# A two-layer graph network: GpSimd's tile operations moved to VectorE, target scores spread through DRAM, and half of each graph layer moved into the turn before

## Chip, cores, metric

One Trainium2 chip, one core, all data in float32. The metric is the device time of one execution in microseconds (us).

## The reference

128 graphs of 128 nodes with 256 features. Layer 0 is attention with relation-dependent values (8 heads) and a feed-forward; layer 1 is two graph-attention steps and a feed-forward. Four layer norms in all. What matters here of layer 1:

```python
Wh  = h @ W
e   = leaky_relu(Wh @ a[:F] + swapaxes(Wh @ a[F:], 1, 2), 0.2)   # target score + source score
att = softmax(where(adj > 0, e, NEG), axis=1)
h   = att @ Wh                                                    # done twice, then residual and norm
```

The edge tile has one graph's source nodes on the 128 partitions. A source score is then one number per partition, which an activation takes as its bias. A target score must be laid along the free axis and be the same on every partition: it has to be *spread*. How that is done is one part of the change.

## The kernel before

Four graphs make a group of 512 tokens; the 32 groups run as *turns* in a software pipeline. While one group is in the second feed-forward, the next but one is in projections and attention, and so on. Functions are generators, and an explicit order says after how many feed-forward steps the next piece of another group is issued. TensorE and ScalarE follow that order; VectorE and the rest are placed by the framework's own scheduling.

```python
def normed(t, n, mv=None):                      # statistics on VectorE
    ...
    nc.gpsimd.tensor_tensor(rs, rs, k.mhalf, op=ALU.pow)
    ...
def scaled(y, gr, br, n, o=None):               # 128x1024 each, on GpSimd
    nc.gpsimd.tensor_mul(o, y, over(gr))
    nc.gpsimd.tensor_add(o, o, over(br))
...
# scores(S, p): four times per half of a group
nc.scalar.activation(e[:, s], pss[s], AF.Exp, scale=SCALE)
nc.vector.tensor_mul(pm[:, s], e[:, s], ad[...])             # pm
# attended(S, p): sums over e and pm
nc.tensor.matmul(pav[...], v[:, d0 : d0 + DH], m[:, s, u, c, :], ...)   # m is e, then pm
...
# layer1(S): spread of target scores by matmul
nc.tensor.matmul(pb, wb[:, c, :], yT[:, c, :], ...)           # first graph step, two of these
nc.tensor.matmul(pb[:, b * P : (b + 1) * P], wh[:, b, D + 1 : D + 2].to_broadcast([P, P]),
                 att[:, b, :], start=True, stop=True)         # second graph step, four of these
# edges(): ends with
nc.gpsimd.tensor_mul(s, s, rd[:, :, None].to_broadcast([P, G, P]))
```

Of the kernel before, what the change touches and what calls it, by code (L numbers as in the profile page):

```python
# [9 lines left out]
F32 = mybir.dt.float32  # L10
I32 = mybir.dt.int32
AF = mybir.ActivationFunctionType
ALU = mybir.AluOpType
# [10 lines left out]
P = 128  # L24
# [79 lines left out]
def fast_pass(ctx, tc, a, out):  # L104
# [21 lines left out]
    small = ctx.enter_context(tc.tile_pool(name="small", bufs=4))  # L126
    ps_s = ctx.enter_context(tc.tile_pool(name="ps_s", bufs=4, space=PSUM))
# [74 lines left out]
    NU = D + 3  # L202
    wu = k.tile([P, NCH, NU], "wu")
    wb = k.tile([P, NCH, P], "wb")

    def graph_weights():
# [8 lines left out]
        gw1T = cut(NCH, D)  # L215
        for m in range(NCH):
            pt = mm_tile(f"pgt_{m}")
            for c in range(NCH):
                nc.tensor.transpose(
                    pt[:, c * P : (c + 1) * P], gw1[:, c, m * P : (m + 1) * P], k.ident  # L220
                )
            nc.scalar.copy(gw1T[:, m, :], pt[:, :D])
        yield
        for m in range(NCH):
            pu = mm_tile(f"pgw_{m}")
            for c in range(NCH):
                nc.tensor.matmul(
                    pu[:, : D + 2], gw1T[:, c, m * P : (m + 1) * P], rhs[:, c, :],
                    start=(c == 0), stop=(c == NCH - 1),
                )  # L230
            nc.scalar.copy(wu[:, m, : D + 2], pu[:, : D + 2])
            nc.vector.tensor_copy(wu[:, m, D + 2 :], wa1[:, m, 1:2])
            nc.vector.tensor_copy(wb[:, m, :], wa1[:, m, 0:1].to_broadcast([P, P]))
# [10 lines left out]

    def normed(t, n, mv=None):

        st = small.tile([P, G, 6], F32, tag="st", name="st_" + n)
        if mv is None:
            mv = small.tile([P, G, 2], F32, tag="mv", name="mv_" + n)
        for b in range(G):  # L250
            nc.vector.bn_stats(st[:, b, :], t[:, b, :])  # L251
            nc.vector.bn_aggr(mv[:, b, :], st[:, b, :])
        rs = small.tile([P, G], F32, tag="rs", name="rs_" + n)
        nc.vector.tensor_scalar(rs, mv[:, :, 1], EPS, None, op0=ALU.add)  # L254
        nc.gpsimd.tensor_tensor(rs, rs, k.mhalf, op=ALU.pow)  # L255
        for b in range(G):
            nc.vector.tensor_scalar(  # L257
                t[:, b, :], t[:, b, :], mv[:, b, 0:1], rs[:, b : b + 1],
                op0=ALU.subtract, op1=ALU.mult,
            )  # L260

    def scaled(y, gr, br, n, o=None):
        if o is None:
            o = w3p.tile([P, G, D], F32, tag="res", name="res_" + n)
        nc.gpsimd.tensor_mul(o, y, over(gr))
        nc.gpsimd.tensor_add(o, o, over(br))
        return o
# [15 lines left out]
    def added(t, p, po, res):  # L283

        nc.vector.tensor_add(  # L285
            flat(t[:, 2 * p : 2 * p + 2, :]), po, flat(res[:, 2 * p : 2 * p + 2, :])
        )

    def ffn(S, layer, inT, wa, ba, func, wb_, res):

        n = f"{layer}_{S['g']}"
# [10 lines left out]
        S[f"t{layer}"] = t = w3p.tile([P, G, D], F32, tag="t", name="t_" + n)  # L302
        for p in range(G // 2):
# [10 lines left out]
            added(t, p, po, res)  # L314
            yield

    def in_order(ffn_, *steps):


        for s in steps:  # L320
            if isinstance(s, int):
                for _ in range(s):
                    next(ffn_, None)
            elif callable(s):
                s()
            else:
                next(s, None)
        for _ in ffn_:
            pass

    def scores(S, p):

        qT, kT, ad = S["qT"], S["kT"], S["ad"]
        n = f"{S['g']}_{p}"

        pss = [ps_s.tile([P, 2, NCH, P], F32, tag="s", name=f"ps_{n}_{s}") for s in range(HC)]
        for u in range(2):
            bs = slice((2 * p + u) * P, (2 * p + u + 1) * P)
            for c in range(NCH):
                for s in range(HC):  # L340
                    rows = slice(s * DH, (s + 1) * DH)
                    nc.tensor.matmul(  # L342
                        pss[s][:, u, c, :], kT[rows, c, bs], qT[rows, c, bs],
                        start=True, stop=True,
                    )
        e = w2p.tile([P, HC, 2, NCH, P], F32, tag="e", name="e_" + n)
        pm = w2p.tile([P, HC, 2, NCH, P], F32, tag="pm", name="pm_" + n)
        for s in range(HC):
            nc.scalar.activation(e[:, s], pss[s], AF.Exp, scale=SCALE)  # L349
            nc.vector.tensor_mul(  # L350
                pm[:, s], e[:, s],
                ad[:, 2 * p : 2 * p + 2, None, :].to_broadcast([P, 2, NCH, P]),
            )
        S["e", p], S["pm", p] = e, pm

    def attended(S, p):

        e, pm, oT, g = S["e", p], S["pm", p], S["oT"], S["g"]
        n = f"{g}_{p}"
        pav = ps_av.tile([P, 2, NCH, P], F32, tag="av", name="pav_" + n)  # L360
        pden = ps_av.tile([P, 2, NCH, P], F32, tag="den", name="pden_" + n)
        for s in range(HC):
            nc.tensor.matmul(  # L363
                pden[s * DH : (s + 1) * DH], k.ones, e[:, s], start=True, stop=True
            )
        for u in range(2):
            v = S["v", 2 * p + u]
            for c in range(NCH):
                for r, m in enumerate((e, pm)):
                    for s in range(HC):  # L370
                        d0 = r * D + c * P + s * DH
                        nc.tensor.matmul(  # L372
                            pav[s * DH : (s + 1) * DH, u, c, :],
                            v[:, d0 : d0 + DH], m[:, s, u, c, :],
                            start=(r == 0), stop=(r == 1),
                        )
        den = pden.rearrange("p u c i -> p (u c i)")
        rd = w1p.tile([P, 2, NCH, P], F32, tag="rd", name="rd_" + n)
        nc.vector.reciprocal(rd, pden)  # L379
        for u in range(2):  # L380
            bs = slice((2 * p + u) * P, (2 * p + u + 1) * P)
            nc.vector.tensor_mul(oT[:, :, bs], pav[:, u], rd[:, u])
        nc.vector.tensor_reduce(c_att[:, 0, g, p : p + 1], den, AX.X, ALU.min)
        nc.vector.tensor_reduce(c_att[:, 1, g, p : p + 1], den, AX.X, ALU.max)

    def projections(S):

        g, xt, ad, xr = S["g"], S["xt"], S["ad"], S["xr"]
        n = str(g)
        nc.gpsimd.tensor_add(xr, xr, over(bo))  # L390

        scr = w2p.tile([P, G, P], F32, tag="gs", name="scr_" + n)
# [3 lines left out]
        )  # L396
        for o, w, bias in (("qT", wq, bq), ("kT", wk, bk)):
# [20 lines left out]

    def attention(S):
# [3 lines left out]
        scores(S, 0)  # L423
        yield
        attended(S, 0)
        scores(S, 1)
        yield
        attended(S, 1)
        yield
        S["t0"] = t = w3p.tile([P, G, D], F32, tag="t", name="t_0_" + n)  # L430
        for p in range(G // 2):
# [8 lines left out]
            added(t, p, po, S["xr"])  # L440
            yield

    def edges(pb, bias, S, l):

        n = f"{S['g']}_{l}"
        s = w2p.tile([P, G, P], F32, tag="gs", name="gs_" + n)
        for b in range(G):
            nc.scalar.activation(  # L448
                s[:, b, :], pb[:, b * P : (b + 1) * P], AF.Identity, bias=bias(b)
            )  # L450
        nc.vector.scalar_tensor_tensor(s, s, ALPHA, s, op0=ALU.mult, op1=ALU.max)  # L451
        nc.scalar.activation(s, s, AF.Exp)
# [9 lines left out]
        nc.gpsimd.tensor_mul(s, s, rd[:, :, None].to_broadcast([P, G, P]))  # L462
        return s

    def layer1(S):



        n, yT = str(S["g"]), S["x2T"]
# [9 lines left out]
        pb = ps_av.tile([P, T], F32, tag="den", name="pb_" + n)  # L479
        for c in range(NCH):  # L480
            nc.tensor.matmul(pb, wb[:, c, :], yT[:, c, :], start=(c == 0), stop=(c == NCH - 1))  # L481
        yield
        att = edges(pb, lambda b: wh[:, b, D + 2 : D + 3], S, 0)
        yield
        yh = w1p.tile([P, G, D + 1], F32, tag="yh", name="yh_" + n)
        pb = ps_av.tile([P, T], F32, tag="av", name="pb2_" + n)
        for b in range(G):
            py = ps_s.tile([P, T], F32, tag="s", name=f"py_{n}_{b}")
            nc.tensor.matmul(  # L489
                py[:, : D + 1], att[:, b, :], wh[:, b, : D + 1], start=True, stop=True  # L490
            )
            nc.scalar.copy(yh[:, b, :], py[:, : D + 1])
            nc.tensor.matmul(  # L493
                pb[:, b * P : (b + 1) * P], wh[:, b, D + 1 : D + 2].to_broadcast([P, P]),
                att[:, b, :], start=True, stop=True,
            )
        att = edges(pb, lambda b: yh[:, b, D : D + 1], S, 1)
        yield
        S["t2"] = t = w3p.tile([P, G, D], F32, tag="t", name="t_2_" + n)
# [473 lines left out]
```

## Time and profile before

| | before |
|---|---|
| median time | 3084.3 us (3 runs, 3083.71 to 3085.99) |
| span of the profiled run | 3083.0 us |
| TensorE, VectorE, GpSimd busy | 3007.7, 1478.7, 895.5 us |
| one turn (start of `pb` to the next) | 94.87 us |

The engine lines, the chain of waits, TensorE's waits and two timelines are shown in the prediction below.

### The profile page before, as it was taken

How to read it: one execution, taken by the hardware profiler on the slowest of the kernel's cores; microseconds unless marked ns; L12 is line 12 of the kernel's file. 1: busy time of each engine (PE TensorE's matmuls, PEld its weight loads, DVE VectorE, ACT ScalarE, POOL GpSimd, SP SyncE). 2: the span in 40 equal slices, each digit the busy share in tenths (PEclk: the TensorE clock that was granted, in tenths of full speed). 3: DMA queues.
4: the chain of work that ended last, by engine and by line, in shares of the span. 5: the costliest groups of instructions: out<-in, count | busy, mean ns of one | idle time of the engine just before them, and what ended most of it. 6: DMA issues, size and time to landing. Idle time of an engine off the chain costs nothing.

```text
span 3083.0 us, 39531 instructions
## 1 busy us (share of the span) xinstructions
PE 3007.7 (98%) x16526; PEld 1981.4 (64%) x16526; DVE 1478.7 (48%) x3445; ACT 998.4 (32%) x1735; POOL 895.5 (29%) x489
## 2 busy tenths in 40 slices
PE   8999999999999999999999999999999999999998
PEld 4666666666666666666666666666666666666665
DVE  4445543455544455444554345553445544455433
ACT  2333333333333333333333333233333333333332
POOL 1233232232232322323323223223232232332332
PEclk9999999999999999999999999999999999999999
DMA  5000000000000000000000000000000000000000
GB/s 159 18 21 18 25 18 18 21 25 18 18 23 19 21 18 18 25 18 21 18 25 18 18 21 25 18 18 23 20 21 18 18 25 18 21 18 11 8 8 15
DMA packets 58136, 69.59 MB, mean 23 GB/s; under 512 B 6752, under 2 KB 44768, under 8 KB 57952
## 3 DMA queue, kind: packets, MB, share of 16 engines
q1 hardware_dynamic: 57120, 66.61, 7.1%
q8 instruction: 131, 2.15, 0.3%
q10 hardware_dynamic: 832, 0.40, 0.0%
q14 instruction: 53, 0.43, 0.0%
HBM read 50.22 MB, written 16.78 MB: 22 GB/s over the span
## 4 chain that ended last, share of the span: by engine, by line
PE 90%; DVE 7%; DMA 1%; ACT 1%; POOL 0%; issue 0%; SPq 0%; ACTq 0%; DVEq 0%; POOLq 0%
PE po L308 29%; PE ph L296 28%; PE pq L402 7%; DVE pm L350 7%; PE pw L474 4%; PE pv L412 4%; PE pav L372 3%; PE pwo L436 3%; PE ps L342 2%; PE pt L275 2%; PE py L489 2%; PE pb L481 2%; PE pg L504 2%; PE pden L363 1%; PE pb L493 1%; ACT e L349 1%
## 5 line engine op out<-in xcount | busy, mean ns | idle before, releaser
L255 POOL TENSOR_TENSOR rs<-rs,mhalf 128x4 f32<-128x4 f32 x127 | 129.1, 1016 | 1274.7 <-DVE rs L254 1274.7
L296 PE MATMUL ph<-yT,w_L_gnn_w_ff 128*128 128x512 f32 x1024 | 462.5, 600 | 0.4 <-ACT hT L300 0.4
L296 PE MATMUL ph<-yT,w_L_gnn_W 128*128 128x512 f32 x1024 | 451.7, 592 | 3.8 <-ACT hT L300 3.4
L308 PE MATMUL po<-w_L_gnn_W,hT 128*128 128x256 f32 x2048 | 453.5, 379 | 0.0
L308 PE MATMUL po<-w_L_gnn_w_ff,hT 128*128 128x256 f32 x2048 | 452.5, 379 | 0.0
L308 PEld LDWEIGHTS po<-w_L_gnn_W,hT 128*128 128x128 f32 x2048 | 386.5, 190 | 64.8 <-issue 15.0
L308 PEld LDWEIGHTS po<-w_L_gnn_w_ff,hT 128*128 128x128 f32 x2048 | 386.7, 190 | 52.2 <-issue 1.0
L296 PEld LDWEIGHTS ph<-yT,w_L_gnn_W 128*128 128x128 f32 x1024 | 194.2, 190 | 235.8 <-issue 227.0
L296 PEld LDWEIGHTS ph<-yT,w_L_gnn_w_ff 128*128 128x128 f32 x1024 | 189.9, 190 | 213.4 <-issue 205.8
L350 DVE TENSOR_TENSOR pm<-e,adj 128x512 f32<-128x512 f32 x256 | 293.2, 1203 | 35.3 <-ACT e L349 35.3
L451 DVE SCALAR_TENSOR_TENSOR gs<-gs 128x512 f32<-128x512 f32 x64 | 44.6, 697 | 533.1 <-ACT gs L448 533.0
L300 ACT ACTIVATE hT<-ph,c_L_gnn_b 128x512 f32<-128x512 f32 x256 | 175.7, 687 | 379.0 <-PE ph L296 378.9
L300 ACT ACTIVATE hT<-ph,c_L_gnn_b_ff 128x512 f32<-128x512 f32 x256 | 176.4, 690 | 372.7 <-PE ph L296 372.7
L285 DVE TENSOR_TENSOR t<-po,res 128x512 f32<-128x512 f32 x128 | 88.5, 691 | 422.6 <-PE po L308 422.6
L462 POOL TENSOR_TENSOR gs<-gs,gr 128x512 f32<-128x512 f32 x64 | 66.7, 1042 | 699.0 <-DVE gr L461 699.0
L379 DVE RECIPROCAL rd<-pden 128x512 f32<-128x512 f32 x64 | 214.4, 3350 | 70.8 <-PE pden L363 70.8
L412 PE MATMUL pv<-wv,xT 128*128 128x512 f32 x512 | 238.7, 599 | 0.8 <-DVE v L416 0.8
L278 ACT ACTIVATE yT<-pt,c_L_gnn_beta,c_L_gnn_g 128x512 f32<-128x512 f32 x128 | 92.7, 774 | 434.6 <-PE pt L275 434.5
L349 ACT ACTIVATE e<-ps 128x512 f32<-128x512 f32 x256 | 132.2, 602 | 217.8 <-PE ps L342 217.8
L251 DVE BATCH_NORM_STATS2 st<-t 128x6 f32<-128x256 f32 x508 | 192.4, 415 | 7.4
L257 DVE TENSOR_SCALAR t<-t,mv,rs 128x256 f32<-128x256 f32 x384 | 132.7, 409 | 112.1 <-POOL rs L255 112.1
L372 PE MATMUL pav<-pm,v 128*32 128x128 f32 x2048 | 132.1, 273 | 40.4 <-DVE pm L350 40.4
(110 smaller groups left out, 3697.8 us busy)
## 6 DMA issues: line engine op xcount, KB each, us to landing
xT<-in_xT_dram SPq DMA_DIRECT2D x32, 512.0 KB, 3.7
x<-in_x_dram SPq DMA_DIRECT2D x32, 512.0 KB, 3.8
out_dram<-t SPq DMA_DIRECT2D x31, 512.0 KB, 2.9
adj<-in_adjT_dram SPq DMA_DIRECT2D x32, 256.0 KB, 2.7
w_L_gnn_W<-in_L_gnn_W_dram SPq DMA_DIRECT2D x2, 1024.0 KB, 7.6
w_L_gnn_w_ff<-in_L_gnn_w_ff_dram SPq DMA_DIRECT2D x2, 1024.0 KB, 8.7
wv<-in_L_gnn_Wv_dram SPq DMA_DIRECT2D x2, 256.0 KB, 5.2
temp<-in_L_gnn_W_dram SPq DMA_DIRECT2D x2, 256.0 KB, 5.8
```

The lines of the kernel that those rows point to most:

```text
L251: nc.vector.bn_stats(st[:, b, :], t[:, b, :])
L255: nc.gpsimd.tensor_tensor(rs, rs, k.mhalf, op=ALU.pow)
L257: nc.vector.tensor_scalar(t[:, b, :], t[:, b, :], mv[:, b, 0:1], rs[:, b : b + 1], op0=ALU.subtract, op1=ALU.mult,)
L296: nc.tensor.matmul(ph, wa[:, c, f * P : (f + 1) * P], inT[:, c, :], start=(c == 0), stop=(c == NCH - 1),)
L300: nc.scalar.activation(hT[:, f, :], ph, func, bias=ba[:, f : f + 1])
L308: nc.tensor.matmul(po[:, s * D : (s + 1) * D], hT[:, f, b * P : (b + 1) * P], wb_[:, f, :], start=(f == 0), stop=(f == NF - 1),)
L349: nc.scalar.activation(e[:, s], pss[s], AF.Exp, scale=SCALE)
L350: nc.vector.tensor_mul(pm[:, s], e[:, s], ad[:, 2 * p : 2 * p + 2, None, :].to_broadcast([P, 2, NCH, P]),)
L372: nc.tensor.matmul(pav[s * DH : (s + 1) * DH, u, c, :], v[:, d0 : d0 + DH], m[:, s, u, c, :], start=(r == 0), stop=(r == 1),)
L379: nc.vector.reciprocal(rd, pden)
L402: nc.tensor.matmul(pq, w[:, c, m * P : (m + 1) * P], xt[:, c, :], start=(c == 0), stop=(c == NCH - 1),)
L412: nc.tensor.matmul(pv, xt[:, c, b * P : (b + 1) * P], wv[:, c].rearrange("p r d -> p (r d)"), start=(c == 0), stop=(c == NCH - 1),)
```

## The change

The intent: take the broadcast products off TensorE; take all tile work off GpSimd, beside which VectorE's `pm` is slow (the prediction shows it), and give it to VectorE; and arrange VectorE by hand so that it copes. The core of the diff:

```diff
+    dram = ctx.enter_context(tc.tile_pool(name="dram", bufs=2, space=bass.MemoryType.DRAM))
-    NU = D + 3
+    NU = D + 4                                  # the target score as one more column of the product
-    wb = k.tile([P, NCH, P], "wb")
...
+    def scaled(S, i, p):                        # on VectorE, half a group at a time
+        nc.vector.tensor_mul(o[:, pair(p)], t[:, pair(p)], over(rows[i][0], 2))
+        nc.vector.tensor_add(o[:, pair(p)], o[:, pair(p)], over(rows[i][1], 2))
...
+    def spread(columns, n):
+        pr = ps_av.tile([P, P], F32, tag="den", name="pr_" + n)
+        nc.tensor.transpose(pr[:G, :], columns, k.ident)
+        nc.vector.tensor_copy(line, pr[:G, :])
+        nc.sync.dma_start(hbm, line)                      # 2 KB out
+        nc.sync.dma_start(t, hbm.partition_broadcast(P))  # 256 KB back, same on all partitions
...
-        nc.gpsimd.tensor_mul(s, s, rd[:, :, None].to_broadcast([P, G, P]))
+        nc.vector.tensor_mul(s, s, rd[:, :, None].to_broadcast([P, G, P]))
...
-    with tc.manual_schedule(engines={mybir.EngineType.PE, mybir.EngineType.Activation}):
+    with tc.manual_schedule(engines={ET.PE, ET.Activation, ET.DVE, ET.SP}):
...                                              # steady turn, f1/f2 first/second feed-forward of two groups,
                                                 # l1 graph layer, at attention, pr projections, n0..n3 norms
+    n3, f1, l1, f1, n3, l1, f1, (n3, 2), store, (f1, 2), prepared,
+    (f1, 3), (l1, 2), (f1, 5), l1, n2, (f1, 2), n2, f1, n1,
+    (pr, 2), n1, turned, pr, (n2, 2), pr, turned,
+    l1 = layer1(S1);  pr, l1, n1, pr, n1, l1, (pr, 2)     # the NEXT group's graph layer begins here
+    (f2, 2), l1, f2, l1, f2, at, (f2, 2), at, (f2, 3), at, (f2, 2), at, f2, at, n0, f2, ...
```

GpSimd keeps the power of the norm (128x4).

## The prediction

> **What bounds the kernel now.** I read the page first: its engine shares, its chain of work that ended last. Then the waits of TensorE alone, then the instruction groups by form, then timelines of one turn in mid-run. (A turn is one group of four graphs; there are 32.)
>
> ```profile
> PE 3007.7 (98%) x16526; PEld 1981.4 (64%) x16526; DVE 1478.7 (48%) x3445; ACT 998.4 (32%) x1735; POOL 895.5 (29%) x489
> PE 90%; DVE 7%; DMA 1%; ACT 1%; POOL 0%; issue 0%; SPq 0%; ACTq 0%; DVEq 0%; POOLq 0%
> ```
>
> TensorE is busy 98% of the span, and the chain is TensorE with a small share of VectorE. So only two things can shorten this kernel: matmul time taken away, or the 75 us in which TensorE stands still (3083.0 - 3007.7). The waits of TensorE say where those lie:
>
> ```profile
> PE pav L372 <- DVE pm L350: 40.4, 62, 1.1
> PE pt L275 <- DVE t L257: 11.1, 3, 6.1
> PE pq L402 <- DMA w_L_gnn_Wq<-in_L_gnn_Wq_dram: 5.9, 1, 5.9
> PE pflag L639 <- DVE good L637: 5.6, 1, 5.6
> ```
>
> The first comes back in nearly every turn (62 of 64 attention halves); the rest are the start, the end and three places without neighbouring work. Why does `pm` come late? It is the product of exponentials and adjacency, 128x512, four in a row per half. Its shortest is 674 ns, its median 680, its longest 2862, its mean 1203. The timelines of VectorE and GpSimd at one such place:
>
> ```profile
> 1501.41 2.48 DVE L350 TENSOR_TENSOR pm<-e,adj 128x512 f32<-128x512 f32 x4
> ...
> 1583.16 6.95 DVE L350 TENSOR_TENSOR pm<-e,adj 128x512 f32<-128x512 f32 x4 [1.02 <-ACT e L349]
> ...
> 1583.38 2.79 POOL L266 TENSOR_TENSOR res<-res,r_L_gnn_b_ln 128x1024 f32<-128x1024 f32 x1
> 1586.13 2.83 POOL L266 TENSOR_TENSOR res<-res,r_L_gnn_beta 128x1024 f32<-128x1024 f32 x1
> ```
>
> With GpSimd idle, four take 2.48 us; with two GpSimd additions on the same stretch they take 6.95 us, and the additions themselves stretch from 2.36 us to 2.8. TensorE pays there 1.12 + 0.19 us. A second look, for the matmuls that the change removes, on TensorE's timeline of the same turn:
>
> ```profile
> 1543.25 3.66 PE L474 MATMUL pw<-wu,yT 128*128 128x259 f32 x16
> 1546.75 1.88 PE L481 MATMUL pb<-yT,wb 128*128 128x512 f32 x4
> 1548.47 3.60 PE L296 MATMUL ph<-yT,w_L_gnn_W 128*128 128x512 f32 x8
> ...
> 1558.81 0.60 PE L489 MATMUL py<-wh,gs 128*128 128x257 f32 x2
> 1559.24 0.38 PE L493 MATMUL pb<-gs,wh 128*128 128x128 f32 x2
> 1559.46 0.60 PE L489 MATMUL py<-wh,gs 128*128 128x257 f32 x2
> ...
> 1571.78 1.89 PE L504 MATMUL pg<-yh,gs 128*128 128x256 f32 x8
> 1573.51 3.60 PE L402 MATMUL pq<-xT,w_L_gnn_Wk 128*128 128x512 f32 x8
> ```
>
> Take starts, not durations, since neighbours overlap. Each logical f32 matmul is two records.
>
> **What the Trainium skill says.** "SBUF — State Buffer", section "Who interferes with whom": a VectorE instruction with two SBUF inputs contends with a GpSimd instruction that reads SBUF; whoever starts first holds the pair for the whole instruction. `pm` and the GpSimd additions are such instructions, and 2.48 against 6.95 us agrees in direction; the GpSimd side was stretched only from 2.36 to 2.8. "GPSIMD Engine Reference", section "4.1 Engine selection": elementwise work on a tile belongs on VectorE, GpSimd being about 2 times slower with two inputs. The trace has 2.35 us for 128x1024 on GpSimd against two 128x512 of 0.62 to 0.68 us on VectorE: 1.7 to 1.9 times. "DMA: Bandwidth & Descriptors", section "Anatomy of one DMA — SWDGE (gpsimd) path": a transfer has a fixed cost of about 2.0 us, most of it the receipt of the write. Here the queue is SyncE's, but the trace is near: 1.8 us from issue to landing for the 128 KB output pieces, 2.7 us for 256 KB of adjacency.
>
> **The change, part by part.**
>
> *Removed: broadcast of target scores.* The product with a spread column `wb` (four records) goes from 1546.75 to 1548.47: 1.72 us per turn, 55.0 us in 32 turns. The second, in layer two, sits between the `py`: the four pairs take 1558.81 to 1561.43 = 2.62 us, while the like-shaped `pg` alone takes 1571.78 to 1573.51 = 1.73 us; so 0.89 us per turn, 28.5 us. The group sums of the page (60.1 and 49.2 us) are larger because they count overlaps; I do not use them. Sum: **-83.5 us**.
>
> *Added on TensorE.* Two transposes per turn of a 128x4 column block. The eight `pt` transposes in the same trace take 1528.62 to 1529.50, 0.11 us each; so 64 x 0.11 = 7 us, and I allow 2 us for the lone small weight load. One more column in `pw` and `py`: 768 records x about 0.85 ns (0.437 us per 512 columns) = 0.7 us. Sum: **+10 us**.
>
> *GpSimd tile operations to VectorE.* GpSimd keeps only the tiny power (128x4). Then nothing holds `pm` back: I expect four in 2.5 us everywhere, and the 40.4 us of waiting go: **-40.4 us**, if the order leaves no other wait there. VectorE's load: 2 (bias) + 16 (four norms, two halves, multiply and add) + 2 (edge normalisation) = 20 instructions of 128x512 per turn, 640 in all, x 0.62 to 0.68 us = about 410 us, plus 64 small copies of about 0.2 us = 13 us; saved in `pm`: 293.2 - 64 x 2.48 = 134 us. New sum 1478.7 + 423 - 134 = about 1768 us, 59% of the span. On average far from binding; it costs nothing unless a burst makes TensorE wait.
>
> *Target scores through DRAM.* Per layer: transpose 0.11, copy 0.2, two transfers one behind the other with issue (0.4 each): 1.8 + 2.7 + 0.8, about 5.6 us altogether. Cover on TensorE in the new order: layer one has two projection steps and two feed-forward steps before the edges, 4 x 1.72 = 6.9 us; layer two has six feed-forward steps, 10.3 us. Hidden, but layer one with only 1.3 us to spare, and VectorE must have copied promptly: its queue then holds a scaling and a `v` addition.
>
> *Order fixed on VectorE and SyncE; first graph layer a turn earlier.* No work is added. The edge chains (score, exponential, mask, normalise) get their feed-forward neighbours; normalised tiles are prepared a few steps before the transposes. Tightest is attention: from scores to the transposes of its norm I count some 24 us of VectorE work (pm 2 x 2.5, reciprocal 2 x 3.35, products and reductions 2 x 2.0, three additions with statistics 3 x 1.75, norm with power 2.9) inside about 30 us of matmuls. I allow 0.2 us of new wait per turn: **+6 us**. The end: in the last turn the second edge chain and its norm stand with less beside them (spread 5.6 plus chain about 6 against three steps 5.2; then a norm); I allow **+5 us**. The start has one gain (one adjacency check no longer stands inside the first norm) and one risk (graph weights in fixed order ahead of the first `v`): 0.
>
> Sum: 3084.3 - 83.5 + 10 - 40.4 + 6 + 5 = **2981 us**; per steady turn, 94.87 us (between two `pb` starts, 313.37 and 408.24) become about 91.4.
>
> **The rivals.**
> (a) *VectorE's fixed order turns into new waits.* In the kernel before, VectorE was free to be arranged otherwise and still served TensorE everywhere but in one place. With 20 more instructions per turn and an 80% full attention stretch (24 of 30 us), a late `pm`, or sum buffers freed late by the reductions (there is one of each), could cost 0.7 us per turn: 2981 + 16 = about 2997; with 1.5 us, about 3022. For: the estimate of the stretch. Against: `pm` is ahead of reciprocals in the new order.
> (b) *The DRAM route is exposed.* If the two transfers take 8 us rather than 5.3, ScalarE, which works in order, stands at the edges and its outputs free the two feed-forward accumulators late. About 1.5 us per turn after its slack is eaten: again about 3020.
> (c) *The matmuls removed were cheaper than they look, or the wait merely moves to other late `pm`.* If the 40.4 us stay, as ScalarE's exponentials or the chain in front take the blame: about 3020. Against: the longer pm coincide with GpSimd instructions.
> (d) *All is covered*, no new wait and a quiet end: about 2966.
>
> **Range and chances.** The removal of 73 us net of matmul time is arithmetic on a saturated engine, and alone gives 3011, 2.4% faster. To stay within 2% (above 3022.6), the waits would have to be 42 us longer than my sum has them: rivals (b) or (c) in full, or two together. I keep most weight between (d) and the mild (a): predicted 2981 us, range 2961 to 3008; faster by over 2%: 0.91, within 2%: 0.08, slower: 0.01.
>
> **What would show each step.** In the changed profile: TensorE's busy sum near 2935 us with share 98 to 99%; no group for `pb`, and 64 transposes into `pr` of about 0.1 us spacing; `pm` mean near 680 ns with longest below 1 us; wait of `pav` for `pm` below 10 us; GpSimd below 150 us busy, nearly all power; VectorE 1.7 to 1.8 ms; SyncE's two transfers for each spread landing in 2 and 3 us; ScalarE not waiting for a transfer at the edges. The prediction is wrong if `pm` stays above 1 us without GpSimd work beside it, if TensorE's waits name VectorE for over 40 us in sum, or if ScalarE's wait for the spread tile shows up each turn.

## More of the kernel before

One more view belongs here: busy time in a stretch in mid-run. The columns are length, then busy us (and instructions) of PE, PEld, DVE, ACT and POOL, then granted clock, DMA share and GB/s. TensorE stands still for 3.93 us in 300 us (300.00 - 296.07), by the records.

```profile
900.00:1200.00 300.00, 296.07 (x1605) 195.12 (x1604) 147.48 (x354) 96.27 (x168) 87.97 (x49) 1.00 0.07 20
```

## The result

The median fell from 3085.1 us (the 3 runs above and a fourth, 3083.71 to 3085.99) to 2958.99 us (4 runs, 2958.13 to 2959.66). The ratio is 0.9591, 95% interval 0.9575 to 0.9608. Ratios here are the mean time of one kernel's fast runs over that of the other's of the same rounds, so not quite the ratio of the medians. The gain is 126 us. I had forecast 103 (2981 us, range 2961 to 3008): right direction, but 2 us below my range.

The page of the changed kernel, engine lines and chain:

```profile
PE 2913.6 (99%) x16206; PEld 1921.8 (65%) x16206; DVE 1804.7 (61%) x4139; ACT 984.1 (33%) x1733; POOL 132.2 (4%) x137
PE 97%; DVE 2%; DMA 0%; issue 0%; ACT 0%; POOL 0%; ACTq 0%; DVEq 0%; POOLq 0%
```

The waits of TensorE in the changed kernel (for whom: us in total, times, longest):

```profile
PE pt L253 <- DVE t L291: 10.7, 4, 4.3
PE pq L393 <- DMA w_L_gnn_Wq<-in_L_gnn_Wq_dram: 6.0, 1, 6.0
PE pg L568 <- DVE gs L533: 5.3, 1, 5.3
PE pflag L682 <- DVE good L680: 4.9, 1, 4.9
PE pden L447 <- DVE c_att L472: 4.7, 2, 3.2
```

`pav` waiting for `pm` is gone; what is left lies at the start and the end: between 170 and 2864 us no wait of TensorE is listed. In a stretch of 300 us in mid-run it has no recorded gap at all, although VectorE does 43 us more in it than in the stretch of 300 us shown for the kernel before:

```profile
1000.00:1300.00 300.00, 300.00 (x1702) 201.39 (x1701) 190.18 (x432) 98.97 (x175) 14.11 (x14) 1.00 0.08 25
```

The shape of `pm` (VectorE, tile view: shortest, median and longest of 256), before and then after:

```profile
L350 DVE TENSOR_TENSOR pm<-e,adj x256: 674/680/2862, 24.8 to 2926.5; 128x512 f32<-128x512 f32 x128
```

```profile
L435 DVE TENSOR_TENSOR pm<-e,adj x256: 679/684/693, 26.3 to 2809.6; 128x512 f32<-128x512 f32 x128
```

A turn now takes 90.38 us (start of `pr` for `wh` at 256.51 and at 346.89) against 94.87. I had said 91.4. So the missing microsecond is inside each turn. The timelines of TensorE at the attention sums of one late half before show where. The columns are start, length, line, operation, tiles, and in brackets the recorded wait:

```profile
1587.83 0.40 PE L372 MATMUL pav<-e,v 128*32 128x128 f32 x8
1588.05 0.39 PE L372 MATMUL pav<-pm,v 128*32 128x128 f32 x4
1589.56 0.41 PE L372 MATMUL pav<-pm,v 128*32 128x128 f32 x2 [1.12 <-DVE pm L350]
1590.16 0.30 PE L372 MATMUL pav<-pm,v 128*32 128x128 f32 x1 [0.19 <-DVE pm L350]
...
1591.81 1.17 PE L342 MATMUL ps<-qT,kT 32*128 32x128 f32 x32
```

and at a like half after, where nothing waits:

```profile
1547.70 0.40 PE L456 MATMUL pav<-e,v 128*32 128x128 f32 x8
1547.92 0.40 PE L456 MATMUL pav<-pm,v 128*32 128x128 f32 x8
...
1549.56 3.72 PE L342 MATMUL po<-w_L_gnn_w_ff,hT 128*128 128x256 f32 x16
```

From the first `pav` to the next other work it is 1591.81 - 1587.83 = 3.98 us before and 1549.56 - 1547.70 = 1.86 us after: 2.12 us lost per late half. The brackets hold only 1.12 + 0.19 = 1.31 us. The rest is hidden: a `pav` matmul is drawn 273 ns long, while in a free run eight of them start within 0.22 us, so each wait is recorded only from the drawn end of the matmul in front of it. (The 62 waits of the list are two in each of 31 late halves; the other half of each turn takes 1.86 us in both kernels.) I added these start-to-start times over all attention halves: 185.3 us before, 121.9 us after. **The late `pm` cost 63.4 us, not the 40.4 us that the list of waits shows.**

The Trainium skill has this, and I had not looked there: "Perfetto Trace Analysis", section "Tensor Engine Instruction (MATMUL, LD_WEIGHTS)", says that the end of a TensorE instruction is estimated from its size and not observed, so its time is a model. The traces here agree, and 23 us hung on it.

### The profile page after: what moved, and what is told of

It reads as the page before. It is cut to its first block, busy times and chain, and to the rows that moved or that the text cites. A ratio compares the mean times of both kernels' runs of the same rounds, so it can differ in the third digit from the quotient of the medians.

```text
span 2957.8 us, 39390 instructions
## 1 busy us (share of the span) xinstructions
PE 2913.6 (99%) x16206; PEld 1921.8 (65%) x16206; DVE 1804.7 (61%) x4139; ACT 984.1 (33%) x1733; POOL 132.2 (4%) x137
## 4 chain that ended last, share of the span: by engine, by line
PE 97%; DVE 2%; DMA 0%; issue 0%; ACT 0%; POOL 0%; ACTq 0%; DVEq 0%; POOLq 0%
PE ph L331 30%; PE po L342 30%; PE pv L403 7%; PE pq L393 7%; PE pw L544 4%; PE pav L456 4%; PE pwo L494 4%; PE pt L253 3%; PE ps L421 2%; PE pden L447 2%; PE py L556 2%; PE pg L568 2%; DMA temp<-in_L_gnn_a_dram 0%; PE pr L504 0%; DVE rd L462 0%; DMA r_L_gnn_bo<-in_L_gnn_bo_dram 0%
## 5 line engine op out<-in xcount | busy, mean ns | idle before, releaser
L342 PE MATMUL po<-w_L_gnn_w_ff,hT 128*128 128x256 f32 x2048 | 470.3, 381 | 0.0
L407 DVE TENSOR_TENSOR v<-pv,r_L_gnn_bv 128x512 f32<-128x512 f32 x128 | 87.7, 686 | 219.9 <-PE pv L403 219.9
L277 DVE BATCH_NORM_STATS2 st<-t 128x6 f32<-128x256 f32 x512 | 210.2, 410 | 8.8
L397 ACT ACTIVATE qT<-pq,c_L_gnn_bq 128x512 f32<-128x512 f32 x64 | 44.0, 688 | 436.4 <-PE pq L393 436.4
L435 DVE TENSOR_TENSOR pm<-e,adj 128x512 f32<-128x512 f32 x256 | 159.6, 685 | 5.2 <-ACT e L427 5.1
L403 PEld LDWEIGHTS pv<-wv,xT 128*128 128x128 f32 x512 | 92.5, 190 | 93.6 <-issue 88.4
```

The lines of the kernel that those rows point to most:

```text
L277: nc.vector.bn_stats(st[:, s, :], t[:, 2 * p + s, :])
L342: nc.tensor.matmul(po[:, s * D : (s + 1) * D], hT[:, f, b * P : (b + 1) * P], wb_[:, f, :], start=(f == 0), stop=(f == NF - 1),)
L403: nc.tensor.matmul(pv, xt[:, c, b * P : (b + 1) * P], wv[:, c].rearrange("p r d -> p (r d)"), start=(c == 0), stop=(c == NCH - 1),)
L435: nc.vector.tensor_mul(pm[:, s], S["e", p][:, s], S["ad"][:, pair(p), None, :].to_broadcast([P, 2, NCH, P]),)
```

## The experiments

The theory: the gain is matmul time removed (about 73 us) plus the full delay of `pm` (63 us), less some microseconds at the ends; the other parts of the change gain nothing by themselves but keep the two from being eaten by new waits. The rivals: the recorded waits are all there was and another part gave the rest; or the order, not GpSimd's absence, cured `pm`. In all eight runs the results were correct. "From 2959" below compares medians with the changed kernel. It was not run again beside the experiments, but the kernel before was: its medians there were 3085.3 us (experiments 1 to 4) and 3083.92 us (5 to 8), against 3085.1. So a difference of about 1 us between rounds means nothing.

### 1. The kernel before, GpSimd's tile work to VectorE, nothing else

```diff
-        nc.gpsimd.tensor_mul(o, y, over(gr))
-        nc.gpsimd.tensor_add(o, o, over(br))
+        nc.vector.tensor_mul(o, y, over(gr))
+        nc.vector.tensor_add(o, o, over(br))       # also the bias and the edge normalisation
```

> The kernel before with only one part of the change: scaling, bias and edge normalisation moved from GpSimd to VectorE, everything else (matmuls, order, free placement on VectorE) as before. Theory A (the cost of a late pm is more than TensorE's recorded idle: between two pav matmuls the records hide it, and the start-to-start length of the pav stages shows 63 us lost in all): 3085 - 63 = about 3022 us, every pav stage 1.86 us long. Rival B (the recorded idle of 40.4 us is all of it, and another part of the change gave the rest): about 3045 us. Rival C (the extra VectorE work makes new waits): 3050 us or more.

Measured: 3072.63 us, ratio 0.9958 (0.9942 to 0.9975). TensorE's waits:

```profile
PE pv L412 <- DVE v L416: 47.8, 30, 1.9
...
PE pav L372 <- DVE pm L350: 0.4, 2, 0.2
```

A came true for the `pav` stages, C for the total. The stages fell to 121.3 us in sum, 64 us less, with the recorded wait down by only 40.0: the matmuls and TensorE's order are exactly those of the kernel before, so this is the direct measure of the hidden part. But about 51 us came back (64 less the 13 won) as a new wait: on VectorE the scalings, four instructions of 1.22 us in a row, now stand in front of the additions into `v`:

```profile
1573.29 1.23 DVE L265 TENSOR_TENSOR res<-t,r_L_gnn_g_ln 128x1024 f32<-128x1024 f32 x1
1574.44 1.22 DVE L265 TENSOR_TENSOR res<-t,r_L_gnn_g 128x1024 f32<-128x1024 f32 x1
1575.57 1.22 DVE L266 TENSOR_TENSOR res<-res,r_L_gnn_b_ln 128x1024 f32<-128x1024 f32 x1
1576.71 1.22 DVE L266 TENSOR_TENSOR res<-res,r_L_gnn_beta 128x1024 f32<-128x1024 f32 x1
1577.84 1.28 DVE L416 TENSOR_TENSOR v<-pv,r_L_gnn_bv 128x512 f32<-128x512 f32 x2
```

### 2. The changed kernel, the same work back on GpSimd

```diff
-        nc.vector.tensor_mul(o[:, pair(p)], t[:, pair(p)], over(rows[i][0], 2))
+        nc.gpsimd.tensor_mul(o[:, pair(p)], t[:, pair(p)], over(rows[i][0], 2))   # and the rest alike
```

> The changed kernel with the same tile operations back on GpSimd, order fixed as after. If GpSimd work as such costs the 63 us, it returns: about 3022 us with pav stages near 4 us in each turn. Rival: in the new order the scalings stand some 10 us ahead of the first pm, so GpSimd is idle by then and little returns: 2960 to 2985 us with pm near 0.7 us; then the order alone would have removed the wait.

Measured: 3018.55 us, 59.6 us from 2959. The total is what I wrote for the first case, but not for its reason. The `pav` stages grew only from 121.9 to 141.3 us (one half a turn, mostly 2.0 to 2.8 us); the rest is other waits of TensorE for VectorE, the norm's `pt` for one (41 times, against 4). A likely reason, not tested apart, is that GpSimd takes about 1.3 us for a 128x512 scaling that takes VectorE 0.68 to 0.69, and that what follows on VectorE comes late. So the new order alone takes away a good part of the collision with `pm` (19 us of it are left, of 63), but GpSimd work in this pipeline costs 60 us anyway.

### 3. The changed kernel, target scores spread by matmul again

```diff
-        target = spread(wh[:, :, D + 3], n + "_0")
+            nc.tensor.matmul(pb..., wb[:, c, :], yT[:, c, :], ...)               # into pb, used as target
-        target = spread(yh[:, :, D + 1], n + "_1")
+            nc.tensor.matmul(pb[:, b, :], wh[:, b, D + 1 : D + 2].to_broadcast([P, P]), S["att"][:, b, :], ...)
```

> The changed kernel with the target scores spread by matmul as before (product with wb, and product with a broadcast column), no DRAM route; order as after. If the removed matmuls were worth their start-to-start time, 1.72 + 0.89 us less 2 x 0.11 us of transposes per turn: +76 us, about 3035 us. If waits hid part of them or the DRAM route costs something: less than +76.

Measured: 3030.79 us, 71.8 us from 2959, against 76 expected. TensorE has no steady wait here either. A turn in mid-run takes 92.78 us, against 90.39 in the changed kernel: 2.39 us, just what was expected per turn. So the removed products are worth what their start-to-start times say, within 4 us over the whole kernel, and the DRAM route costs next to nothing in the new order.

### 4. The kernel before, only the DRAM route added

> The kernel before with only the target scores turned and spread through DRAM; GpSimd and order as before. Matmul time -76 us. If the order was needed to hide the route (spread about 5.6 us and edge chain about 5.5 us against 10.3 us of neighbouring matmuls, and ScalarE standing at the edges): 1 to 2 us of new wait per turn, 3040 to 3070 us. If the route is hidden in the old order too: about 3010 us.

The edit is the `spread` of the diff above, put in the place of the two products. Measured: 3160.39 us, ratio 1.0242 (1.0225 to 1.0259): 75 us *slower* than before, and worse than I expected. TensorE's work shrank as planned; its waits grew:

```profile
PE pav L372 <- DVE pm L350: 74.4, 59, 2.3
PE ph L296 <- ACT hT L300: 23.0, 3, 11.2
PE pr L446 <- ACT wh L490: 14.9, 32, 0.5
PE pr L446 <- ACT yh L501: 14.9, 32, 0.5
...
PE py L498 <- POOL gs L474: 9.3, 30, 0.7
PE pg L510 <- POOL gs L474: 8.6, 31, 1.6
```

`pm` collides with GpSimd for longer (the `pav` stages sum to 229.8 us); the transposes `pr`, which this edit puts right behind the products, wait for ScalarE's copies; and some 28 of the 75 us lie in the last two turns and the end (the 23.0 us for `hT` among them). The same route that costs next to nothing after is a loss here. GpSimd's work and VectorE's free placement are still those of before, so this run does not show which of them, or the order of TensorE's steps, makes the difference.

### 5. The changed kernel, VectorE and SyncE placed freely again

```diff
-    with tc.manual_schedule(engines={ET.PE, ET.Activation, ET.DVE, ET.SP}):
+    with tc.manual_schedule(engines={ET.PE, ET.Activation}):
```

> The changed kernel with only the placement given back: VectorE and SyncE free to be arranged as in the kernel before, TensorE and ScalarE as in the change. The first experiment (GpSimd work moved in the old, free arrangement) won 64 us in the pav stages and lost some 50 us to a new wait of pv for the addition into v. If the fixed order on VectorE is what avoids such waits: 2985 to 3020 us, with a new wait of TensorE for VectorE in each turn. If the order of TensorE's own steps is what avoids them: within 10 us of 2959.

Measured: 2978.42 us, 19.4 us from 2959, between the two expectations. There is one new wait per turn, of 0.7 us by the records (a turn takes 91.31 us, against 90.39):

```profile
PE pq L393 <- DVE t L274: 19.5, 29, 1.0
```

So the fixed order on VectorE and SyncE is worth 19 us. The `v` wait of experiment 1 did not return without it. Something else of the change removed that one: TensorE's own new order, or the scalings in halves (two of 0.68 us for one of 1.22); the two were not separated.

### 6. The changed kernel, useless GpSimd work beside `pm`

```diff
+        if p == 0:
+            e0 = flat(S["e", 0][:, 0]...)
+            for j in range(10):
+                nc.gpsimd.tensor_add(junk, e0[:, :224], e0[:, 224:448])
```

> The changed kernel, where GpSimd has ten useless additions of 128x224 on its own tile to do beside the first four pm of each turn (a small tile of the DRAM route is moved to a pool with two buffers to make room). Results stay right. If reading by GpSimd beside pm is what stretches pm: pm of the first half well above 0.9 us, pav stages of the first half longer than 1.86 us. Theory A (records hide part of a late pm): the time grows by the growth of the pav stages, about one and a half times the recorded idle of pav. Rival B: it grows by the recorded idle alone. Rival C: pm stays at 0.68 us; then contention isn't the cause.

Measured: 2996.86 us, 37.9 us from 2959. `pm` beside that work took about 1.1 us:

```profile
L440 DVE TENSOR_TENSOR pm<-e,adj x256: 676/1143/1248, 24.7 to 2849.1; 128x512 f32<-128x512 f32 x128
```

Apart from the buffer of one small tile, nothing but GpSimd's additions was changed, so GpSimd's work beside it stretches `pm`. The `pav` stages grew by 26.9 us (to 148.8), of which 13.7 us are recorded as waits: theory A, here by a factor of 2. The remaining 11 us fit `pden`, which waits for the sums' buffer behind the late VectorE (17.0 us recorded, against 4.7).

### 7. The changed kernel, the whole graph layer in one turn

```diff
-    n3, f1, l1, f1, n3, l1, f1, (n3, 2), store, (f1, 2), prepared, (f1, 3), (l1, 2), (f1, 5), l1, n2, ...
+    n3, l1, f1, l1, f1, n3, f1, (n3, 2), store, (f1, 2), l1, prepared, f1, l1, (f1, 2), l1, f1, l1, (f1, 4), (l1, 2), ...
-    pr, l1, n1, pr, n1, l1, (pr, 2)
+    pr, n1, pr, n1, (pr, 2)
-    (f2, 2), l1, f2, l1, f2, at, ...
+    (f2, 4), at, ...
```

> The changed kernel with the whole graph layer of a group back in one turn, inside the first feed-forward; the rest as after. The same matmuls. Two edge chains (spread 5.6 us and chain 5.5 us each) and a norm then need some 29 us of cover from 27 us of feed-forward steps that also carry them in order, so I expect 2 to 5 us of new wait per turn: 3020 to 3110 us. If moving the first half a turn back bought nothing: within 10 us of 2959.

Measured: 3082.1 us, 123 us from 2959: all of the gain is gone. This is the one schedule of that kind that I tried; a better one may lose less. Both edge chains are now waited for:

```profile
PE 2959.2 (96%) x16206; PEld 1912.8 (62%) x16206; DVE 1796.9 (58%) x4139; ACT 1067.0 (35%) x1793; POOL 132.3 (4%) x137
...
PE py L556 <- DVE gs L533: 42.6, 30, 1.4
PE pg L568 <- DVE gs L533: 22.7, 31, 5.3
```

Compare the first line with the changed kernel's: the same 16206 matmul records at the same mean clock (0.994), yet TensorE is "busy" 45.6 us longer. The likely reason is again waiting drawn as work: four waits a turn are recorded in mid-run, and an estimate from these numbers is 45.6 / 120, some 0.4 us hidden in each.

### 8. A version that beats both

```diff
+        if S["g"] == NG - 1:                     # last group only: spread by matmul, into `target`
...
-    f2, l1, f2, l1, (f2, 5), l1, l1, (f2, 2), l1, f2, l1, (f2, 3), l1, l1, l1,
+    f2, l1, f2, l1, (f2, 5), l1, l1, (f2, 2), l1, l1, l1, f2, l1, f2, l1,
-    in_order((n2, 2), lambda: turned(S1, 2), ...
+    in_order(n2, f2, n2, f2, lambda: turned(S1, 2), ...
```

> A version meant to beat both: the last group's second graph layer has nothing left to hide the DRAM route, so there, and only there, the target scores are spread by matmul (0.9 us), and two feed-forward steps are kept to stand beside the norm after it. Waits of 5.3 us (pg) and 3.9 us (pt) at the end, and some 2 us of lowered clock behind them, should fall to about 2 us: 2950 to 2954 us against 2959. If the end's waits are only moved: no difference.

Measured: 2946.51 us (5 runs, 2946.26 to 2948.69), ratio to the kernel before 0.9557 (0.9544 to 0.9570): 12.5 us less than the changed kernel (11.3 if each is taken from the kernel before in its own rounds), more than I expected. One stretch near the end, columns as in the first stretch shown; first the changed kernel, then this one, which is some 10 us further on in its work there:

```profile
2900.00:2920.00 20.00, 11.95 (x25) 6.60 (x26) 14.21 (x44) 2.99 (x5) 2.02 (x2) 0.66 0.00 0
```

```profile
2900.00:2920.00 20.00, 18.31 (x53) 9.20 (x53) 12.33 (x36) 6.94 (x10) 2.01 (x2) 1.00 0.08 27
```

The same matmuls in both, the last `pg` and the last 32 `ph`; first the changed kernel, then this one:

```profile
2904.17 3.78 PE L568 MATMUL pg<-yh,gs 128*128 128x256 f32 x8 [5.34 <-DVE gs L533]
...
2914.13 16.02 PE L331 MATMUL ph<-yT,w_L_gnn_w_ff 128*128 128x512 f32 x32
```

```profile
2896.29 1.96 PE L576 MATMUL pg<-yh,gs 128*128 128x256 f32 x8 [1.43 <-DVE gs L533]
...
2905.14 14.00 PE L331 MATMUL ph<-yT,w_L_gnn_w_ff 128*128 128x512 f32 x32 [0.43 <-ACT yT L256]
```

The waits are one part: 5.3 and 3.9 us (for `pg` and `pt`) became 1.4, 1.3 and 0.4. The other is the granted clock, 0.66 in the stretch with the long waits, 1.00 in the one with the short: the same `pg` took 3.78 against 1.96 us, the same `ph` 16.02 against 14.00. The Trainium skill, "TensorE: Matmul & The Clock Gate", section "What's actually happening", says that the clock let through depends on how busy the array has been recently; these lines agree. At this kernel's end, a long wait is paid for twice.

This run made two edits, and experiment 3 tells something of one. It too spreads the last group's scores by matmul, but in the changed kernel's order, and its end waits just as long:

```profile
2978.29 3.75 PE L582 MATMUL pg<-yh,gs 128*128 128x256 f32 x8 [5.43 <-DVE gs L535]
```

So the spread by matmul alone shortens nothing there; the gain needs the moved feed-forward steps. Whether these suffice without it was not run.

## Why the prediction was wrong, and where it was right

| term of the sum | predicted | measured | by what |
|---|---|---|---|
| products removed, transposes added | -73.5 us | -71.8 | experiment 3 |
| `pm` no longer late | -40.4 | -63.4 | `pav` stages, 185.3 to 121.9; experiment 1: 64 |
| new waits per turn | +6 | 0 | no wait listed from 170 to 2864 us |
| start and end | +5 | about +9 | what is left of -126.1 |

**The step that failed** is the one that put the late `pm` at 40.4 us: "Then nothing holds `pm` back [...] and the 40.4 us of waiting go". The mechanism was right; the size was taken from the column of recorded waits, where it should have been taken from starts. I had written, for the removed products, "Take starts, not durations, since neighbours overlap", and then did not do so for the wait. I also misread the 62 waits as 62 of 64 attention halves; they are two in each of 31. So the list put one delay at 1.31 us, where it was 2.12. The gap of 23.0 us in this term is as large as the whole miss (2981 - 2959 = 22 us). The same error is behind "the 75 us in which TensorE stands still" and behind "TensorE's busy sum near 2935": the sum fell to 2913.6 because the busy time of before held waiting.

**Rival (d)**, no new wait, is what happened in mid-run, though even it was put at 2966, with the same mis-sized term. (Its sum is not shown; without the two allowances for waits my own terms give 2970.)

**Right, but cheaper or dearer than said.** VectorE's 1804.7 us against 1768 was near. The DRAM route of about 5.6 us was right where nothing stands in its way: in experiment 4 the transpose and ScalarE's start at the edges lie 4.9 to 5.5 us apart in nearly all of 64. In the changed kernel it is 7.8 to 9.5 us in the first graph step of the turns in mid-run. In one of them the transpose starts at 1522.31 and ScalarE at the edges at 1531.48; VectorE's copy waited 2 us in its queue, as I had feared, and the read back took 4.8 us. Its median there is 4.3 us, against the 2.7 that I assumed. The record points to why: the next group's three loads are issued right behind that read. The two traced reads near the end without these loads take 3.2 us; with no load behind it (experiment 4), or at most one (experiment 5), the read takes 3.0 to 3.1. From the pages of the changed kernel, experiment 4 and experiment 5; the last number is the median from issue to landing in us:

```profile
spread<-hbm SPq DMA_DIRECT2D x64, 256.0 KB, 4.3
```

```profile
spread<-hbm SPq DMA_DIRECT2D x64, 256.0 KB, 3.0
```

```profile
spread<-hbm SPq DMA_DIRECT2D x64, 256.0 KB, 3.1
```

Rival (b)'s premise, 8 us for the two transfers, was not met: the write takes 1.2 us and the read 4.3. The longer route cost TensorE nothing that the records show, since the wait stayed on ScalarE, and even there it was 16.3 us in 20 of 64 times: in the new order ScalarE has that slack.

**GpSimd and VectorE.** The chain of events in the late half agrees with an exclusive lock, more strictly than I had read it. The four `pm` together take 6.95 us; by the single records the second ends at 1586.72, 0.55 us after the first GpSimd addition (1586.17), and the third at 1589.51, 0.55 us after the second (1588.96). In experiment 6, too, each `pm` beside an addition ends 0.55 us after it. GpSimd's own lengthening, 2.36 to 2.8 us, fits a wait for a `pm` that had started first.

**The order.** I had called it "no work is added" and booked only risks. The experiments show that the gains hang on it: in the old order the move off GpSimd alone is worth 13 us and the DRAM route alone costs 75 us, and with both in, but the graph layer in one turn (experiment 7), nothing is left of 126. Both together in the old order were not run. With GpSimd's work moved and the new order, but no DRAM route (experiment 3), the kernel is 54.5 us faster than before.

**Still open.** The +9 us at start and end is a remainder and not measured term by term; experiment 8 shows 12.5 us to be had at the end. How the 60 us of experiment 2 and the 75 us of experiment 4 divide among their causes was not separated.

## What to carry to other kernels

On a saturated TensorE, measure what a wait costs from start to start against a place without the wait; the recorded idle and the busy share both hide a part of each wait, here some 0.4 us (0.81 us in two waits). Before crediting a change with work taken off the critical engine, ask which order makes room for what is put elsewhere: here two good ideas were worth 13 us and minus 75 us alone, and 126 us together and in a new order. When a pipeline is full in mid-run, look at its last turn, where there is little left to hide behind and, here, the clock fell too (0.66).

## What the Trainium skill lacked or had wrong

- "Perfetto Trace Analysis" says that TensorE's recorded ends are estimated, but not what follows for waits: 62 short waits recorded as 40.4 us cost 63.4 us, and the same 16206 matmuls were recorded as busy for 2913.6 or 2959.2 us.
- "DMA: Bandwidth & Descriptors", section "Anatomy of one DMA — SWDGE (gpsimd) path", gives a fixed cost of about 2.0 us plus bytes over bandwidth, fitted on another kind of queue; for 256 KB that is an estimate of 2.6 us. Here, on SyncE's queue, the 2 KB write took less: 1.21 us in the median of 64 (1.17 to 2.08), from its issue to the issue of the read that waits for it. The read of 2 KB spread to 128 partitions took 3.0 us in the median with nothing issued beside it (30 landings traced in experiment 4), and 4.3 us (3.3 to 4.9, 29 traced) in the changed kernel with three loads right behind. The page says that a source may repeat, but has no time for it.
- "SBUF — State Buffer" on the shared port was right: `pm` beside GpSimd took up to 2.86 us, and in the changed kernel, without it, at most 0.693.
